# Weights read back in single pieces, two products reordered, and one eviction moved, in a one-core hybrid block

## The chip, the cores and the metric

The kernel runs on one core of a Trainium2 chip. The metric is the device time of one execution in microseconds (us); the time of a kernel is the median of its runs. A core has five engines with queues of their own: PE (TensorE, matrix products; its weight loads are listed as PEld), DVE (VectorE), ACT (ScalarE), POOL (GpSimd) and SP (SyncE, which here only issues transfers). Each engine takes its instructions in the order in which they stand; semaphores order the engines among each other. Products land in PSUM, eight banks of 128 partitions x 512 float32, and have to be copied or added out of it by ACT or DVE before a bank is used again.

## The reference

Everything is float32. The input x is 2 x 2048 x 256. Four residual layers follow each other, each on a layer norm of x:

1. a gated scan: an RMS norm and a 256 x 768 projection give q, kv and a; then s_t = sigmoid(a_t) s_(t-1) + kv_t along the 2048 rows, and q * s is added to x;
2. a feed-forward layer 256 -> 1024 -> 256 with an exact GELU and weights rounded to three values (W1, b1, W2, b2);
3. attention of second order with 16 heads of 64 (q, k, v = x W_q, x W_k, x W_v, each 256 x 1024), a recurrence over the rows, for each head

```
G   = G + k_t (k_t C)        S_K = S_K + k_t k_t'
C   = C + q_t v_t'           o_t = q_t (S_K C - G)
```

   and o W_o is added to x;
4. the feed-forward layer of 2 again, with the same weights.

## The kernel before

The 4096 rows are 32 chunks of 128. The kernel has three parts. `front` does layers 1 and 2 in blocks of four chunks. `attention` does layer 3, and in its last two steps works off the first block of layer 4. The last loop does the rest of layer 4.

**The order** of PE, DVE, ACT and POOL is written out by hand: inside `tc.manual_schedule(engines=by_hand)` an engine's instructions stand in the order in which the Python code makes them. SP's transfers are ordered likewise by when they are made in these parts. Nothing else plans.

**Attention.** A step s is one chunk of one of the two sequences; NS is 32. Steps with even s are `first` (sequence 0), odd s sequence 1; n = s // 2 is the chunk, and `more` is false in the last two steps, 30 and 31. The recurrence is worked chunk by chunk in two stages. `inter` (L887) and `intra` (L901) with q and the running sum S give uT; `products` (L870), masked by DVE (L876), gives the part inside the chunk; `update` (L927) adds the chunk to the running sums S and M; a second `inter` and `intra` with M give oT, two steps later; `outward` (L948) is o W_o, added to x. Stage two needs u also in the other orientation, uN. It is made by DVE's 32 x 32 transposes, a trip through DRAM by SP (`units_out`: one transfer of 512 KB; `turn_rows`: four of 128 KB back), and a copy by ACT (`units_end`, L967, line name uN). kT is made from k in the same way (`keys_out`, `turn_rows`, `turn_end`). All these products have 64 x 64 tiles on PE: one `inter`, `intra` or `products` is 64 matmuls and 64 weight loads.

`evict` (L912 and L914) copies uT or oT out of its two banks with three copies: one of 128 partitions, two of 64. Its argument names the engine, ACT if none is given.

**Seven.** The projections q, k and v of the two sequences' next chunks are done together by Strassen's scheme with seven products, class `Seven`. `go(i)` issues product i and what belongs to it. Three banks are used, X, Y and Z:

| go | bank | after the product |
|---|---|---|
| 2 | Y | |
| 1 | X, new | ACT copies X to C11 |
| 0 | | DVE adds Y to C11 |
| 5 | Z, new | ACT copies Z to C22 |
| 6 | X | ACT copies X to C12 |
| 7 | X | DVE adds X to C22 |
| 3 | Z | DVE adds Z to C12 |
| 4 | X | ACT copies X to C21 |

So 7 waits until ACT has copied what 6 left in X, and 4 until DVE has added what 7 left there. X and Z of q come from a ring of two banks called uT, which uT's own sums use too; those of v from the ring oT; k of step 0 on from uT. Y and all other sums of attention come from a ring of four.

**The weights back.** Layer 4 needs the rounded W1, W2 and their Strassen sums again. `front` wrote them to DRAM, and `ffn_weights_back` reads them with 14 transfers of 256 KB: four for w1 and three for w1_s (`weights(True)`), four for w2 and three for w2_t3 (`weights(False)`). They go over the freed space of wk, wk_t, wv and wv_t and are issued on ACT's queue (L387; names w_back, w_s_back, w_t_back). Each call of `last.part()` issues the next one; `last.part(None)` issues all that are left of the present group. A step has four calls of `last.part()`: before `outward` of step s-3, before the update, in the middle of the second half, and at the end. `weights(True)` stands at the end of step 28, `weights(False)` at the end of step 29.

In steps 30 and 31 `fill(2)` and `fill(1)` put products of layer 4 (L433) between attention's. In step 31 `units(31)` turns u by PE and DVE instead of the trip through DRAM, and uN of step 30 is copied by ACT before the update of M.

Of the kernel before, what the change touches and what calls it, by code (L numbers as in the profile page):

```python
# [43 lines left out]
def kernel(  # L44
# [701 lines left out]
    def attention(keep, pool, state, last):  # L746
# [9 lines left out]
        act, dve = nc.scalar.copy, nc.vector.tensor_copy  # L756
# [105 lines left out]
        def products(s, left, nm):  # L862


            b, n = steps[s]
            banks = [bank([P, NPR, CH], f"h{nm}{b}_{n}_{h}") for h in range(2)]
            for p in range(NPR):
                for c in range(2):
                    for h in range(2):
                        nc.tensor.matmul(  # L870
                            banks[h][halves[c], p, :], lhsT=d[s][left][halves[h], p, halves[c]],
                            rhs=d[s]["qT"][halves[h], p, halves[c]], start=True, stop=True,
                        )
            d[s][nm] = pool.tile([P, 2, NPR, CH], FP, tag=nm, bufs=1, name=f"{nm}{b}_{n}")
            for h in range(2):
                nc.vector.tensor_tensor(d[s][nm][:, h], banks[h], mask8, ALU.mult)  # L876

        def inter(s, sums, nm):

            b, n = steps[s]  # L880
            banks = [bank([P, NPR, CH], f"h{nm}{b}_{n}_{c}", nm) for c in range(2)]
            for p in range(NPR):
                for c in range(2):
                    if d[s][sums][c] is None:
                        continue
                    for h in range(2):
                        nc.tensor.matmul(  # L887
                            banks[c][halves[h ^ c], p, :], lhsT=d[s][sums][c][halves[h], p, :],
                            rhs=d[s]["qT"][halves[h], p, halves[c]],
                            start=(p == 0), stop=False, skip_group_check=True,  # L890
                        )
            d[s][nm + "b"] = banks
# [15 lines left out]
        def evict(s, nm, copy=act):  # L908
            b, n = steps[s]
            banks = d[s][nm + "b"]  # L910
            t = pool.tile([P, NPR, P], FP, tag=nm, bufs=2 if nm == "uT" else 1, name=f"{nm}{b}_{n}")
            copy(t[:, :, halves[0]], banks[0])  # L912
            for h in range(2):
                copy(t[halves[h], :, halves[1]], banks[1][halves[h ^ 1], :, :])  # L914
            d[s][nm] = t
# [47 lines left out]
        def turn_end(s, nm):  # L963

            b, n = steps[s]
            t = pool.tile([P, NPR, P], FP, tag=nm, bufs=1, name=f"{nm}{b}_{n}")
            act(t, d[s]["r" + nm].rearrange("p t q -> p q t"))  # L967
            d[s][nm] = t

        def keys_out(s):  # L970
            turn_squares(s, "kT", d[s]["kN"].rearrange("t (q b i) -> t b q i", q=NPR, b=NQ))
# [4 lines left out]
        def units_end(s):  # L976
            turn_end(s, "uN")
            d[s]["uN"] = d[s]["uN"].rearrange("p a e -> p (a e)")
# [9 lines left out]
        NS = len(steps)  # L988
        pair_sums(0)
        stats = norm_stats(norm_pool, pair(1), bias=True)  # L990
        k, q, v = Seven(0, "kN", "oT"), Seven(0, "qT", "uT"), Seven(0, "vN", "oT")
# [18 lines left out]
        update(0, "kN", "kN", "S")  # L1010
        v.go(6)
        turn_end(0, "kT")
        v.go(7, 3)
        for s in range(NS):
            first, n = s % 2 == 0, s // 2
            more = n + 1 < CPB
            inter(s, "S", "uT")
            products(s, "kT", "p1")
            if first and n + 2 < CPB:
                stats = norm_stats(norm_pool, pair(n + 2), bias=True)  # L1020
            elif s == NS - 4:
                last.stats()
            elif s == NS - 2:
                last.second_stats()
            if s == 0:
                v.go(4)
                pairs[1] = norm_turned(norm_pool, pair(1), xn, bufs=1)
                pair_sums(1)
            if s % 2 == 1 and more:
                q, v = Seven(n + 1, "qT", "uT"), Seven(n + 1, "vN", "oT")  # L1030
            if s == 1:
                q.go(2)
                v.go(2)
                keys_out(s + 1)
            elif s % 2 == 1 and s + 1 < NS:
                keys_out(s + 1)
            if s == 2:
                k = Seven(n + 1, "kN", "uT")
                k.go(2)
            if first and s > 0:  # L1040
                units_end(s - 1)
            last.part()
            if s >= 3:
                outward(s - 3, 1)
            intra(s, "S", "kN", "p1", "uT")
            if s >= 2:
                intra(s - 2, "M", "vN", "p2", "oT")
            if s + 1 < NS:
                turn_rows(s + 1, "kT")
            evict(s, "uT")  # L1050
            if not more:
                if s >= 2:
                    evict(s - 2, "oT")
                last.begin(first)
                fill = last.fill
                fill(2)
                if not first:
                    units_end(s - 1)
                    units(s)
                fill(2)  # L1060
            elif first:
                if s != 2:
                    k = Seven(n + 1, "kN", "uT")
                    k.go(2)
                k.go(1)
                if s >= 2:
                    evict(s - 2, "oT")
                else:
                    units_out(s)
                    turn_rows(s, "uN")  # L1070
                k.go(0, 5)
            else:
                if s >= 2:
                    evict(s - 2, "oT", dve)
                    units_end(s - 1)
                units_out(s)
                turn_rows(s, "uN")
                if n + 2 < CPB:
                    raw = norm_squares(pool, pair(n + 2), [xn], 2, "xraw", 1)
                if s > 1:  # L1080
                    q.go(2)
                    v.go(2)
                q.go(1)
                v.go(1)
                q.go(0, 5)
                v.go(0, 5)
                q.go(6)
                v.go(6)
                if s == 1:
                    units_end(s - 1)  # L1090
            last.part()
            if s == NS - 1:
                last.second_rows()
            if s + 1 < NS:
                update(s + 1, "kN", "kN", "S")
            if s >= 1:
                update(s - 1, "uN", "vN", "M")
            if s == NS - 1:
                update(s, "uN", "vN", "M")
            if first and not more:  # L1100
                turn_end(s + 1, "kT")
            if not more:
                fill(2)
            elif first:
                k.go(*((6, 3, 7) if s > 0 else (6, 7, 3)))
            else:
                v.go(7)
                q.go(7)
                v.go(3, 4)
                q.go(3)  # L1110
            last.part()
            if first and s > 0:
                units_out(s)
            if more:
                turn_end(s + 1, "kT")
            if s >= 1:
                inter(s - 1, "M", "oT")
                products(s - 1, "uT", "p2")
            if not more:
                fill(1)  # L1120
            elif first:
                k.go(4)
                if n + 2 < CPB:
                    xn = norm_rows(norm_pool, pair(n + 2), stats)
                else:
                    last.rows()
            else:
                q.go(4)
            if not first and s + 2 < NS:
                keys_out(s + 2)  # L1130
            if first and s > 0:
                turn_rows(s, "uN")
            if not first and n + 2 < CPB:
                xnT = norm_pool.tile([P, ND, B * P], FP, tag="xnT", bufs=1, name=f"xnT{n + 2}")
                pairs[n + 2] = norm_end(raw, xnT)
                pair_sums(n + 2)
            elif s == NS - 3:
                last.turned()
            if s == NS - 4:
                last.weights(True)  # L1140
            elif s == NS - 3:
                last.part(None)
                last.weights(False)
            last.part()
            if s >= 2:
                outward(s - 2, 0)
        last.out()
# [18 lines left out]
    def pair(n):  # L1166
        return [b * CPB + n for b in range(B)]
# [10 lines left out]
    class Last:  # L1178
# [60 lines left out]
        def fill(self, n):  # L1239
            run(self.steps, n)  # L1240
# [29 lines left out]
    with tc.tile_pool(name="keep", bufs=3) as keep_pool:  # L1270
        with (
# [4 lines left out]
            last = Last(keep_pool, attn_pool)  # L1276
# [68 lines left out]
```

## Time and profile before

| | us |
|---|---|
| median of 3 runs | 1224.65 (1224.0 to 1228.08) |
| profiled execution, its own time | 1226.85 |
| profiled span, first to last instruction | 1224.3 |
| PE busy in the span | 1207.6 |
| DVE, ACT, POOL busy | 785.7, 602.8, 224.9 |

Mean granted clock of PE over the span: 0.999. The front runs to about 308 us, attention from there to about 1038, the rest of layer 4 to the end. Times in the text are microseconds from the span's start. In a row of a timeline the first number is the start, the second the duration, and the bracket at the end is how long the engine had been idle before, and what ended that. In a row of waits the numbers are the total, the count and the longest. "issue" as releaser means that the profile shows nothing that the engine waited for. ACTq and SPq are the queues' own sequencers, issuing transfers.

### The profile page before, as it was taken

To read this page: it belongs to the slowest core of one execution; us is meant where nothing else is said; L and a number is where in the kernel's file an instruction comes from. 1 tells how busy PE (TensorE), PEld (TensorE's weight loads), DVE (VectorE), ACT (ScalarE), POOL (GpSimd) and SP (SyncE) were. 2 spreads that over 40 slices of the span, in tenths; PEclk is the share of its full clock that TensorE was granted. 3 is DMA by queue.
4 is the path that set the end of the run, shared out by engine and by line. 5 is a ranking of instruction groups with operands and counts; after the bars stand their busy time and mean duration, and the time that the engine had idled before them with its cause. 6 is when DMAs were issued, how large, how long until landed. Compare 5 with 4: busy or idle time off the path is not lost.

```text
span 1224.3 us, 46435 instructions
## 1 busy us (share of the span) xinstructions
PE 1207.6 (99%) x21132; PEld 965.6 (79%) x21132; DVE 785.7 (64%) x1283; ACT 602.8 (49%) x953; POOL 224.9 (18%) x363
## 2 busy tenths in 40 slices
PE   9999999999989999999999999999999989999998
PEld 6588777999667777777777777777777878999998
DVE  7966654665466666667666666756766645667764
ACT  4355544453355545454554544455455543455542
POOL 3742143322101100110110011011011100322340
PEclk9999999999999999999999999999999999999999
DMA  9210000000233343233233324323333531112111
GB/s 323 111 61 1 1 1 1 1 2 1 70 123 103 94 139 121 85 129 125 89 106 131 119 87 141 115 83 122 123 103 94 180 109 46 59 63 76 63 53 35
DMA packets 76115, 106.66 MB, mean 87 GB/s; under 512 B 7792, under 2 KB 61808, under 8 KB 75664
## 3 DMA queue, kind: packets, MB, share of 16 engines
q1 hardware_dynamic: 73392, 99.64, 24.3%
q10 hardware_dynamic: 2448, 3.93, 1.1%
q8 instruction: 165, 2.70, 0.9%
q0 software_dynamic: 80, 0.14, 0.1%
q14 instruction: 30, 0.25, 0.1%
HBM read 55.45 MB, written 48.23 MB: 85 GB/s over the span
## 4 chain that ended last, share of the span: by engine, by line
PE 96%; ACT 1%; issue 1%; DMA 1%; DVE 1%; POOL 0%; SPq 0%; ACTq 0%; DVEq 0%; POOLq 0%
PE ox L524 10%; PE hy L948 10%; PE hx L433 9%; PE pq L311 6%; PE hkN_X L816 5%; PE hp L870 5%; PE hqT_X L811 5%; PE hvN_X L816 5%; PE oz L524 5%; PE hz L433 4%; PE huT L887 3%; PE hoT L887 3%; PE huT L901 3%; PE hS L927 3%; PE hoT L901 3%; PE hM L927 3%
## 5 line engine op out<-in xcount | busy, mean ns | idle before, releaser
L876 DVE TENSOR_TENSOR p<-hp,mask 128x512 f32<-128x512 f32 x128 | 82.2, 683 | 95.6 <-PE hp L870 95.6
L948 PE MATMUL hy<-wo,oT 128*128 128x256 f32 x512 | 123.6, 385 | 0.0
L768 POOL TENSOR_TENSOR S<-xnT 128x128 f32<-128x128 f32 x32 | 14.8, 461 | 531.0 <-ACT xnT L255 513.4
L948 PEld LDWEIGHTS hy<-wo,oT 128*128 128x128 f32 x512 | 93.7, 190 | 18.9 <-issue 6.7
L445 ACT ACTIVATE hT<-hT,b_sb 128x256 f32<-128x256 f32 x192 | 85.4, 500 | 33.1 <-DVE hT L477 31.5
L187 ACT ACTIVATE xn<-x_sb,nb,rs 128x256 f32<-128x256 f32 x124 | 64.8, 591 | 69.1 <-POOL nb L173 69.1
L311 PE MATMUL pq<-xnT,wqkva 128*128 128x512 f32 (+1 forms) x216 | 85.0, 547 | 0.6 <-ACT xnT L215 0.3
L912 ACT COPY uT<-huT 128x512 f32<-128x512 f32 x32 | 18.7, 585 | 127.3 <-PE huT L901 127.3
L311 PEld LDWEIGHTS pq<-xnT,wqkva 128*128 128x128 f32 x216 | 39.9, 190 | 37.9 <-issue 34.7
L937 DVE TENSOR_TENSOR S<-S,hS 128x512 f32<-128x512 f32 x60 | 41.2, 687 | 43.9 <-PE hS L927 40.8
L231 DVE STREAM_TRANSPOSE sqkT<-kN 128x1024 f32<-128x1024 f32 x32 | 65.9, 2058 | 1.3 <-ACT kN L847 1.2
L967 ACT COPY kT<-rawkT 128x1024 f32<-128x1024 f32 x32 | 66.6, 2082 | 0.0
L231 DVE STREAM_TRANSPOSE squN<-uT 128x1024 f32<-128x1024 f32 x31 | 63.6, 2051 | 4.0 <-ACT uT L914 3.5
L967 ACT COPY uN<-rawuN 128x1024 f32<-128x1024 f32 x31 | 64.6, 2084 | 1.9 <-issue 1.2
L410 POOL TENSOR_TENSOR xT<-xnT 128x256 f32<-128x256 f32 x15 | 13.6, 907 | 249.2 <-ACT xnT L217 95.7
L530 DVE TENSOR_TENSOR x_sb<-x_sb,ox 128x256 f32<-128x256 f32 x64 | 26.7, 416 | 48.5 <-PE ox L524 48.5
L155 DVE BATCH_NORM_STATS2 st<-x_sb 128x6 f32<-128x256 f32 x128 | 51.3, 402 | 2.5 <-DMA x_sb<-in_x_dram 2.4
L927 PEld LDWEIGHTS hS<-kN 64*64 64x64 f32 x1984 | 32.7, 134 | 23.2 <-issue 23.1
L847 ACT COPY vN<-hvN_X 128x512 f32<-128x512 f32 x16 | 9.4, 586 | 80.7 <-PE hvN_X L816 80.7
L451 ACT COPY hT<-hx 128x512 f32<-128x512 f32 x32 | 18.6, 581 | 61.7 <-PE hx L433 61.7
L821 DVE TENSOR_TENSOR kN<-kN,hkN_Y 128x512 f32<-128x512 f32 x16 | 11.0, 686 | 54.0 <-ACT kN L830 54.0
L901 PEld LDWEIGHTS huT<-p,kN 64*64 64x64 f32 x2048 | 33.2, 134 | 15.0 <-issue 9.2
(245 smaller groups left out, 2929.8 us busy)
## 6 DMA issues: line engine op xcount, KB each, us to landing
dsqkT<-sqkT SPq DMA_DIRECT2D x32, 512.0 KB, 3.3
rawkT<-dsqkT SPq DMA_DIRECT2D x128, 128.0 KB, 2.9
dsquN<-squN SPq DMA_DIRECT2D x31, 512.0 KB, 3.4
rawuN<-dsquN SPq DMA_DIRECT2D x124, 128.0 KB, 3.2
out_dram<-x_sb SPq DMA_DIRECT2D x16, 256.0 KB, 2.2
x_sb<-in_x_dram SPq DMA_DIRECT2D x7, 512.0 KB, 8.9
dsqxn<-sqxn SPq DMA_DIRECT2D x14, 256.0 KB, 3.7
rawxn<-dsqxn SPq DMA_DIRECT2D x56, 64.0 KB, 2.4
```

Source lines behind the costliest of these rows:

```text
L231: nc.vector.transpose(to, src)
L311: nc.tensor.matmul(pq[:, :nt], lhsT=wqkva[:, d, col : col + P], rhs=xnT[:, d, :], start=(d == 0), stop=(d == ND - 1),)
L433: nc.tensor.matmul(at[a][:, j, :], lhsT=A[:, f * P : (f + 1) * P], rhs=Bm, start=(new and j == 0), stop=True, skip_group_check=True,)
L445: nc.scalar.activation(out, out if src is None else src[:, j, :], AF.Gelu, bias=b1_sb[:, f : f + 1])
L524: nc.tensor.matmul(banks[name][:, c, :], lhsT=A[f // 2][:, f % 2, c * P : (c + 1) * P], rhs=Bm[:, f, :], start=(new and c == 0 and f == 0) ...
L816: nc.tensor.matmul(to, lhsT=self.A[i], rhs=self.B[i], start=new, stop=True, skip_group_check=True)
L876: nc.vector.tensor_tensor(d[s][nm][:, h], banks[h], mask8, ALU.mult)
L887: nc.tensor.matmul(banks[c][halves[h ^ c], p, :], lhsT=d[s][sums][c][halves[h], p, :], rhs=d[s]["qT"][halves[h], p, halves[c]], start=(p = ...
L901: nc.tensor.matmul(banks[c][halves[h ^ c], p, :], lhsT=d[s][nat][halves[c], feats(h, p)], rhs=d[s][pm][halves[c], h, p, :], start=(d[s][su ...
L927: nc.tensor.matmul(banks[c][halves[h], p, :], lhsT=d[s][left][halves[c], feats(h, p)], rhs=d[s][right][halves[c], feats(h, p)], start=True ...
L948: nc.tensor.matmul(py, lhsT=d[s]["oT"][:, p, :], rhs=wo[:, p, :], start=(p == 0), stop=(p == NPR - 1),)
L967: act(t, d[s]["r" + nm].rearrange("p t q -> p q t"))
```

## The change

Five edits, all in `attention`. No instruction is added or taken away in total.

- Before step 0, v's products 7 and 3 swap.
- In step 0, k's product 6 moves from behind the update to in front of it.
- In step 1, `units_end(0)` (ACT's copy of uN) moves in front of the evictions of q and v, where it already is in later odd steps; and product 1 of v now comes before product 1 of q.
- In step 31, `evict` of oT of step 29 is done by DVE. In step 30 it stays on ACT.
- In step 29, two more calls of `last.part()`, and the one at the end of the step now comes before `part(None)` and `weights(False)`. The seven transfers of w1 and w1_s then stand one at the end of step 28 and six in step 29: before `outward`, after product 1 of q and v, after product 6, after product 7, after product 3 and 4 of v, and at the step's end. `part(None)` has none left. The first transfer of w2 then stands in the first half of step 30, ahead of `outward`, and each later one a place later than before.

```diff
@@ before step 0
-        v.go(7, 3)
+        v.go(3, 7)
@@ step, last two
-                if s >= 2:
-                    evict(s - 2, "oT")
+                evict(s - 2, "oT", act if first else dve)
@@ step, first and more
                 k.go(0, 5)
+                if s == 0:
+                    k.go(6)
@@ step, odd and more
                 if s >= 2:
                     evict(s - 2, "oT", dve)
-                    units_end(s - 1)
+                units_end(s - 1)
                 units_out(s)
                 turn_rows(s, "uN")
...
-                q.go(1)
-                v.go(1)
+                for part in (q, v) if s > 1 else (v, q):
+                    part.go(1)
+                if s == NS - 3:
+                    last.part()
                 q.go(0, 5)
                 v.go(0, 5)
                 q.go(6)
                 v.go(6)
-                if s == 1:
-                    units_end(s - 1)
             last.part()
@@ after the updates
-                k.go(*((6, 3, 7) if s > 0 else (6, 7, 3)))
+                k.go(*((6, 3, 7) if s > 0 else (7, 3)))
             else:
                 v.go(7)
                 q.go(7)
+                if s == NS - 3:
+                    last.part()
                 v.go(3, 4)
                 q.go(3)
             last.part()
@@ end of the step
             if s == NS - 4:
                 last.weights(True)
-            elif s == NS - 3:
+            last.part()
+            if s == NS - 3:
                 last.part(None)
                 last.weights(False)
-            last.part()
```

## The prediction

> **What bounds the kernel now.** I read the page's busy times and chain first, then the waits of PE (TensorE), then the timelines of PE and ACT round the longest wait, then the DMA traffic of that stretch. From the page:
>
> ```profile
> span 1224.3 us, 46435 instructions
> ...
> PE 1207.6 (99%) x21132; PEld 965.6 (79%) x21132; DVE 785.7 (64%) x1283; ACT 602.8 (49%) x953; POOL 224.9 (18%) x363
> ...
> q8 instruction: 165, 2.70, 0.9%
> ...
> PE 96%; ACT 1%; issue 1%; DMA 1%; DVE 1%; POOL 0%; SPq 0%; ACTq 0%; DVEq 0%; POOLq 0%
> ```
>
> PE is the bound from end to end. The change removes no matmul, so it can only win PE's idle time, or add to it. The waits of PE list nearly all of that (total, times, longest):
>
> ```profile
> PE huT L901 <- issue: 3.3, 1, 3.3
> PE hM L927 <- ACT uN L967: 2.3, 2, 1.5
> ...
> PE hkN_X L816 <- ACT kN L838: 0.8, 1, 0.8
> PE hvN_X L816 <- ACT vN L838: 0.7, 1, 0.7
> ...
> PE hqT_X L811 <- ACT uT L912: 0.7, 1, 0.7
> ```
>
> A "busy" matmul hides some loss, so I measure loss as start-to-start distance beyond that form's usual one. The longest wait stands in step 30 (s = NS-2):
>
> ```profile
> 979.43 1.15 PE L901 MATMUL huT<-p,kN 64*64 64x64 f32 x62
> 983.91 0.27 PE L901 MATMUL huT<-p,kN 64*64 64x64 f32 x1 [3.33 <-issue]
> ...
> 985.10 1.73 PE L433 MATMUL hy<-xnT,w_back 128*128 128x256 f32 x4
> 986.62 1.91 PE L433 MATMUL hx<-xnT,w_back 128*128 128x256 f32 x4
> 988.33 1.32 PE L433 MATMUL hz<-xT_last,w_s_back 128*128 128x256 f32 x4
> 989.48 1.03 PE L433 MATMUL hx<-xT_last,w_s_back 128*128 128x256 f32 x4
> ```
>
> "issue" means that no semaphore held PE. After it, the 128x256 matmuls up to 988.8 stand 427 ns apart instead of 216; the trace has a granted clock of 0.5 for 3.41 us from 985.49. The stall costs 3.54 us by start-to-start distance and the slow clock half of 3.41, 1.7: 5.2 us.
>
> What was late is PE's own instructions. Queue q8 moved 165 packets of 16,384 bytes; 2 x 21,132 PE instructions over 165 is 256 a packet, so q8 is PE's instruction fetch. In the DMA records its packets start after every 260 or so PE instructions (952.77, 956.38, 966.60, 971.92), but the next starts only at 981.47, after 441. Just before it ACT issued five 256 KB weight loads in 2.3 us, and SP 512 KB at 975.21. ACT's queue, then the DMA queues from 973.3 to 981.4:
>
> ```profile
> 973.87 0.33 ACTq L387 DMA_DIRECT2D w_s_back<-dw_s  x1
> ...
> 974.23 0.93 ACTq L387 DMA_DIRECT2D w_s_back<-dw_s  x2
> 975.20 0.44 ACTq L387 DMA_DIRECT2D w_back<-dw  x1
> ...
> 975.78 0.35 ACTq L387 DMA_DIRECT2D w_back<-dw  x1
> ```
>
> ```profile
> DMA packets 848, 1.82 MB, mean 225 GB/s; under 512 B 90, under 2 KB 90, under 8 KB 847
> ...
> q10 hardware_dynamic: 703, 1.29, 50.6%
> q1 hardware_dynamic: 144, 0.52, 16.0%
> q14 instruction: 1, 0.01, 0.2%
> ```
>
> No q8 packet stands in that stretch: the fetch moved when 1.8 MB had drained. Counting 256 instructions back from where PE ran dry, it was due near 976.5, and came some 5 us late.
>
> **The change, part by part.** All against the profiled span of 1224.3.
>
> *v.go(3, 7).* Before, product 6 is followed by 7 into the same bank X, which ACT must first empty: the matmul at 328.42 is 0.75 us late by start-to-start distance. Product 3 writes bank Z, long evicted, and takes 0.95 us, more than the wait. DVE's two additions swap and end as before. Gain 0.75. If that cover failed the 0.75 would stay.
>
> *k.go(6) before the update in step 0.* Product 7 at 341.10 is 0.88 late for the same reason. Now the update's 64 matmuls (1.09) lie between 6 and 7. But 6 now follows 5 at once: its bank X is emptied by ACT at 337.53, or 336.78 after the first gain, and 6 would start at 337.27, so it does not wait. Late next is product 4: X must be freed by DVE's addition of 7, which now queues behind the two S writes (0.66 and 0.69, ending near 340.9), so about 341.5; 4 could start at 341.3. That takes 0.25 back. Gain 0.63.
>
> *Step 1: units_end(0) early, v before q.* q's first product waited 0.88 for ACT to empty a uT bank (349.83); v's bank is free and its product (0.96) covers that. The M update at 357.97 waited 1.74 for ACT's copy of uN. That copy (2.05) now stands ahead of ACT's copies of v and q, and what is queued behind it on ACT is late: with intra at 346.6 (1.4 earlier), uT's copies end at 349.57, uN at 351.62, v's at 352.15, q's at 352.7. PE reaches q.go(6) at 351.35 and waits 1.45 for that bank. Its uN input is there: its four reads were issued from 341.63 and land in about 3 us. So the two waits (2.62) become about 1.7 (1.45 and 0.2 for the second uT bank). Gain 0.88. Bounds: 0.3 if ACT's copies stretch, 1.7 if it hides more. The 0.93 "issue" wait at 378.2 and the 0.84 before huT at 367.46 (q's last copy) are untouched: 0.
>
> *Seven places a step for the weights.* No load is added; 14 of 256 KB remain. Step 29 now has six ordered places (and step 28's end one), so part(None) finds nothing left. ACT's queue gets an issue after the X copies at 960 (0.33 of sequencer, against copies of 0.58 with 0.3 idle after each: covered; uncovered 0.33), two together near 963.3 (ACT is idle for 5.1 us after), one at 969, one at 974; the first w2 load goes behind the uN copy of step 30. The four loads together at 973.87 to 975.64 held ACT for 1.2 us before uN, which has slack (M uses it at 991). SP's and POOL's queues keep their order; of SP's transfers the step-29 reads of uN share the engines with 0.5 MB more, which at 1.82 MB over 6.6 us (975 to 981.5; 275 GB/s) delays them 1.9 us; in before they land near 970 and are used at 975.8. The w2 loads stand a place or so later; first use 1022.5, over 20 us after.
>
> At PE's next fetch, due at 976.5, the engines then hold w1_s's last load, w2's first and SP's 512 KB: 1.05 MB, not 1.8. If the fetch waits for all of it at 275 GB/s, it starts near 979.2, takes 0.94, and as before (982.41 to 983.91) PE resumes 1.5 later, at 981.6, against a run-dry at 980.55: 1.1 us of stall left. If it slips in, none. I take 0.5, the middle, and no slow clock, because PE's other waits of up to 1.5 us left the granted clock at 1. Gain 5.2 - 0.5 = 4.7.
>
> Two rules of the Trainium skill speak against this step. "Runtime: NRT & Kernel Launch", section on instruction fetch mechanics, has the sequencer fetch the next 256-instruction page while it runs the present one, with the cost mostly hidden; "DMA: Bandwidth & Descriptors", section on queues, rings and completion order, lets each DMA engine take turns between queues packet by packet, so that a fetch passes a long queue after one packet (0.1 us in this stretch). By them the burst can't starve PE: the 5.2 stay, and the sum is 3.1 (1221.6). The row is the packet at 981.47 after 441 instructions; I follow it.
>
> *Last eviction of o by VectorE.* In step 31 ACT copies uT, then oT (1.75), then hx, then uN until 1010.86; M at 1010.91 is 0.93 late. With oT on DVE (idle 4.88 us there; the three copies take 2.08, as its own rows at 956.1 show, and end near 1007.8, before hT's addition), ACT copies hx when it exists (1007.5) and uN until about 1010.1. uN's reads were issued from 1001.30 to 1003.87 and land in 3.2, by 1007. Gain 0.8.
>
> **Sum:** 0.75 + 0.63 + 0.88 + 4.7 + 0.8 = 7.8, a span of 1216.5. The profiled execution took 1226.85, 2.2 above the median of 1224.65; I take the same 7.8 off the median: **1216.9**.
>
> **Rivals.** (1) *The fetch was not late because of this burst, or unprofiled runs do not stall there*: for it, the two rules and the 2.2 us between profiled run and median; against it, the one gap in q8 coincides with the burst. It leaves 3.1: 1221.6, within 0.3%. (2) *ACT is the new wait in step 1 and takes the early gains back*: q.go(6) waits for uN. For it, ACT has no gap left there; against it, the old order waits too. Without the 2.3 of steps 0 and 1: 1224.65 - 5.5 = 1219.1. (3) *The starved fetch moves to step 29*, the other side: the fetch at 966.60 now meets 0.5 MB more. It takes 0.88 + 1.5, and PE runs dry at about 971.2, so it may be 2.2 us late before it costs; my estimate is 1.9. Beyond that each us costs one, and near 3.3 idle the slow clock comes with it. If both this stall and the old one stand at 5.2 each: 1224.65 - 3.1 + 5.2 = 1226.8, slower; with a longer drain past 1228.3.
>
> **How the numbers follow.** About 0.3% (3.7 us) is what a measurement tells from no change. Forecast 0.73 and rival 2 0.09 are both faster, 0.82; rival 1 0.12 is same; rival 3 0.06, of which I put 0.05 in slower and 0.01, the cheaper end, in same: 0.13. Range: low end, 5.2 in full, the step-1 bound of 1.7 and the 0.93 fetch wait gone too make 10.0: 1214.6, rounded down to 1214; high end, rival 1 at 1221.6, rounded to 1222.
>
> **What would show it.** In the changed kernel: no 3 us "issue" wait in huT L901 and no 0.5 clock near 980; q8 packets no more than some 300 instructions apart there; ACTq loads single, but for one pair; no waits of hvN_X or hkN_X on ACT; hM in step 31 late by under 0.2; one wait of hqT_X in step 1 near 1.5. Wrong if a new "issue" wait stands at 966 to 972, or step 1 loses over 2.6.

## The result, and the profile after

The changed kernel takes 1219.2 us (median of 7 runs, 1217.3 to 1222.21), the kernel before 1225.38 (7 runs). The two medians differ by 6.2 us. The ratio estimated from all runs is 0.9955, with an interval of 0.9937 to 0.9974: 5.5 us less, between 3.2 and 7.7. Predicted were 1216.9 and 7.8 less. The direction and the range held, and so did the cause named for each part. One term of the sum, that of the weight loads, was too large for most executions, and the picture of how a fetch waits behind transfers was too simple.

From the page of the profiled execution after (its own time 1222.21, 4.6 below that of before):

```profile
span 1220.2 us, 46432 instructions
...
PE 1207.3 (99%) x21132; PEld 965.2 (79%) x21132; DVE 787.5 (65%) x1286; ACT 601.2 (49%) x950; POOL 224.5 (18%) x363
...
PE 97%; DVE 1%; issue 1%; DMA 1%; ACT 1%; POOL 0%; SPq 0%; DVEq 0%; ACTq 0%; POOLq 0%
```

PE's work is the same to 0.3 us, so nearly all of the change is idle time of PE. Queue q8 again has 165 packets. Three copies went from ACT to DVE, the eviction of oT. The waits of PE (total, times, longest):

```profile
PE hoT L901 <- issue: 3.2, 4, 1.4
PE hqT_X L811 <- ACT qT L830: 1.0, 1, 1.0
...
PE huT L901 <- issue: 0.3, 1, 0.3
...
PE hkN_X L816 <- DVE kN L821: 0.3, 1, 0.3
```

The 3.3 us wait of huT is 0.3, and the waits on ACT's kN, vN, uT and uN are gone. In their place stand the two predicted ones: hqT_X on ACT's copy of q, and hkN_X on DVE. Not predicted is the first line, four waits of PE in step 2 (1.02), at 587 and 807 (0.24 and 0.59), and in step 29 (1.37, near 957). In step 30, PE's timeline, then ACT's queue:

```profile
980.88 1.16 PE L901 MATMUL huT<-p,kN 64*64 64x64 f32 x62
982.38 0.21 PE L901 MATMUL huT<-p,kN 64*64 64x64 f32 x1 [0.34 <-issue]
982.39 0.28 PE L901 MATMUL hoT<-p,vN 64*64 64x64 f32 x3
...
983.52 1.13 PE L433 MATMUL hy<-xnT,w_back 128*128 128x256 f32 x4
```

```profile
975.32 0.33 ACTq L387 DMA_DIRECT2D w_s_back<-dw_s  x1
...
975.87 0.33 ACTq L387 DMA_DIRECT2D w_back<-dw  x1
```

Two loads where five stood. The break comes after the same 62 products: the page of instructions ends at the same place, but the next one is there 0.34 us later instead of 3.33. The four products of hy behind it take 1.13, where on the slow clock they took 1.73; the trace has a granted clock of 1 up to the span's last 1.4 us.

**Where the time went, by stage.** I cut the spans at the starts of PE's first huT product of steps 0, 2, 29, 30 and 31, at the first product of attention and at the last product of `outward`. All values are differences of such starts in one profile each; "after, again" is a second profile of the changed kernel:

| stage | before | after | loads alone | order alone | eviction alone | after, again |
|---|---|---|---|---|---|---|
| start of attention to step 0 | 20.00 | 19.15 | 20.00 | 19.14 | 20.00 | 19.15 |
| steps 0 and 1 | 37.13 | 35.55 | 37.13 | 35.53 | 37.13 | 35.53 |
| steps 2 to 28 | 582.56 | 584.38 | 581.82 | 583.77 | 582.25 | 584.13 |
| step 29 | 25.46 | 27.38 | 27.01 | 25.49 | 25.65 | 25.97 |
| step 30 | 23.99 | 19.43 | 19.66 | 22.48 | 22.55 | 19.21 |
| step 31 to the last `outward` | 37.91 | 36.89 | 37.78 | 37.58 | 37.07 | 36.84 |
| span | 1224.3 | 1220.2 | 1221.3 | 1220.6 | 1223.9 | 1217.3 |

The stages in front of and behind these differ by up to about 3 us between executions without any change there. Two columns from one execution each are therefore to be compared by stage, not by span.

Steps 2 to 28 differ as well, though nothing was changed in them. They took 583.8 to 584.7 us in the four profiles with the changed kernel's order of step 1, and 581.8 to 583.7 in the seven with the old order. Whether a part of the early gain is lost there again these single profiles don't settle.

**What the waits named "issue" are.** In the 14 profiles, PE has 109 waits of more than 0.09 us from step 2 on into step 31 for which the profile shows no releaser. Of these, 102 end 2.1 to 2.8 us after the start of a q8 packet, as the 3.33 us wait did (981.47 to 983.91). That marks nearly all of them as late instruction fetches.

### The profile page after: what moved, and what is told of

It reads as the page before. It is cut to its first block, busy times and chain, and to the rows that moved or that the text cites. A ratio compares the mean times of both kernels' runs of the same rounds, so it can differ in the third digit from the quotient of the medians.

```text
span 1220.2 us, 46432 instructions
## 1 busy us (share of the span) xinstructions
PE 1207.3 (99%) x21132; PEld 965.2 (79%) x21132; DVE 787.5 (65%) x1286; ACT 601.2 (49%) x950; POOL 224.5 (18%) x363
## 4 chain that ended last, share of the span: by engine, by line
PE 97%; DVE 1%; issue 1%; DMA 1%; ACT 1%; POOL 0%; SPq 0%; DVEq 0%; ACTq 0%; POOLq 0%
PE ox L524 10%; PE hy L948 10%; PE hx L433 9%; PE pq L311 6%; PE hp L870 5%; PE hkN_X L816 5%; PE hqT_X L811 5%; PE hvN_X L816 5%; PE oz L524 5%; PE hz L433 5%; PE huT L887 3%; PE hS L927 3%; PE hoT L887 3%; PE huT L901 3%; PE hoT L901 3%; PE hM L927 3%
## 5 line engine op out<-in xcount | busy, mean ns | idle before, releaser
L948 PEld LDWEIGHTS hy<-wo,oT 128*128 128x128 f32 x512 | 93.6, 190 | 19.2 <-issue 7.1
L516 DVE TENSOR_TENSOR hS<-hT 128x512 f32<-128x512 f32 x62 | 41.2, 686 | 5.6 <-ACT hT L445 5.6
```

The lines of the kernel that those rows point to most:

```text
L948: nc.tensor.matmul(py, lhsT=d[s]["oT"][:, p, :], rhs=wo[:, p, :], start=(p == 0), stop=(p == NPR - 1),)
```

## The experiments

A diff starts from the kernel before, unless the text names another. Where no ratio is given, the kernel was executed once, and only its profile is used.

**The loads alone.**

```diff
                 q.go(1)
                 v.go(1)
+                if s == NS - 3:
+                    last.part()
...
                 q.go(7)
+                if s == NS - 3:
+                    last.part()
                 v.go(3, 4)
...
-            elif s == NS - 3:
+            last.part()
+            if s == NS - 3:
                 last.part(None)
                 last.weights(False)
-            last.part()
```

> The kernel before with only the change of the weight loads (two more places in step 29, none left for the end of the step). Theory (late instruction fetch behind the burst): the 3.3 us issue wait of huT in step 30 shrinks to under 1 us and the slow clock near 985 goes; minus 3.1 to 5.2 us, less what a new short fetch wait near 957 costs. Rival (fetch and burst have nothing to do with each other): the wait stays near 3 us in the same place, and the time is within 1 us of before.

Measured: 1222.91 (22 runs), ratio to before 0.9978 (0.9972 to 0.9985), so 2.7 us less, 1.8 to 3.4. PE's waits from 320 to 1036 in its profile:

```profile
PE hM L927 <- ACT uN L967: 2.3, 2, 1.5
PE hoT L901 <- issue: 1.5, 2, 1.2
...
PE hkN_X L816 <- ACT kN L838: 0.8, 1, 0.8
PE hvN_X L816 <- ACT vN L838: 0.7, 1, 0.7
```

The long wait of huT is gone and step 30 takes 19.66 instead of 23.99; the early waits stand as before. This alone makes about half of the gain. But step 29 took 1.5 us more in this profile: the issue wait of 1.2 in hoT, near 957.

**The order alone**, before step 0 and in steps 0 and 1.

```diff
-        v.go(7, 3)
+        v.go(3, 7)
...
+                if s == 0:
+                    k.go(6)
...
-                    units_end(s - 1)
+                units_end(s - 1)
...
-                q.go(1)
-                v.go(1)
+                for part in (q, v) if s > 1 else (v, q):
+                    part.go(1)
...
-                if s == 1:
-                    units_end(s - 1)
...
-                k.go(*((6, 3, 7) if s > 0 else (6, 7, 3)))
+                k.go(*((6, 3, 7) if s > 0 else (7, 3)))
```

> The kernel before with only the new order of products and copies in steps 0 and 1. Theory: minus 2.1 to 2.3 us at the start of step 2; the waits on ACT of hvN_X (328), hkN_X (341), hqT_X (350) and hM (358) are gone, one wait of hqT_X on ACT's copy of q (1.0 to 1.5) and one of hkN_X on DVE (0.3) are new; the wait in step 30 stays. Rival (ACT's copy of uN ahead of the others takes it all back): within 0.5 us at the start of step 2.

Measured: 1222.1 (6 runs), ratio 0.9971 (0.9958 to 0.9984), 3.5 us less, 2.0 to 5.1. By stage it is 0.86 and 1.60, 2.5 together, inside that interval. The burst still stands in this kernel, and so does its wait. PE in step 30:

```profile
977.82 1.16 PE L901 MATMUL huT<-p,kN 64*64 64x64 f32 x62
981.11 0.26 PE L901 MATMUL huT<-p,kN 64*64 64x64 f32 x1 [2.14 <-issue]
...
981.28 1.91 PE L901 MATMUL hoT<-p,vN 64*64 64x64 f32 x61
983.11 1.74 PE L433 MATMUL hy<-xnT,w_back 128*128 128x256 f32 x4
```

Same place and same 62 products, but 2.14 us, not 3.33; the clock was at 0.5 from 980.97 to 984.38, so hoT took 1.91 instead of 1.1. So the slow clock also came with a wait of 2.1 us.

**The eviction alone.**

```diff
-                if s >= 2:
-                    evict(s - 2, "oT")
+                evict(s - 2, "oT", act if first else dve)
```

> The kernel before with only the eviction of oT in step 31 on VectorE. Theory: hM in step 31 no longer waits 0.8 us for ACT's uN; minus 0.8 us there, which is less than the timing's own scatter. Rival (uN's reads from DRAM land too late for it): the wait stays, named after uN's DMA.

Measured: 1223.89 (14 runs), ratio 0.9991 (0.9981 to 1.0002): the runs don't tell it from no change. In the profile hM of step 31 starts 0.20 us late instead of 0.93, and the stage takes 37.07 instead of 37.91. Its huT wait in step 30 was 2.16 us.

**The burst moved to step 28.** All seven loads of w1 and w1_s at the end of step 28.

```diff
             if s == NS - 4:
                 last.weights(True)
+                last.part(None)
```

> The kernel before with all seven loads of w1 and w1_s at once at the end of step 28 (1.8 MB), 26 us earlier than its burst of five. Theory: the late fetch moves with the burst: an issue wait of 3 to 6 us and a slow clock between 951 and 960, none over 1 us near 984. Rival (the wait belongs to step 30, not to the loads): 3 us near 984 as before, nothing new near 955.

Half of the expectation failed. Step 30 did as the theory has it (19.68, clock at 1, an issue wait of 0.2). But near 955 the fetch brought a wait of 0.2 only. ACT's queue:

```profile
948.50 2.27 ACTq L387 DMA_DIRECT2D w_back<-dw  x2
...
950.80 2.04 ACTq L387 DMA_DIRECT2D w_back<-dw  x2
957.14 2.07 ACTq L387 DMA_DIRECT2D w_s_back<-dw_s  x3
959.26 0.58 ACT L912 COPY uT<-huT 128x512 f32<-128x512 f32 x1 [8.21 <-DMA w_s_back<-dw_s]
```

And SP's:

```profile
952.51 1.73 SPq L242 DMA_DIRECT2D rawuN<-dsquN  x4
```

The seven did not go out as one burst: four did, the fifth was held to 957.14. The trace shows by what. Transfers of ACT and SP take turns with the same few semaphores, and an issue waits until the transfer that had its semaphore last has landed. The fifth load has the semaphore of the first of SP's four reads of uN; this landed at 957.12, and the load was issued at 957.14. In the same way the fourth load (952.48) followed SP's store of uN, landed at 952.46, and the sixth (957.88) SP's second read, landed at 957.85.

PE's fetch came 4.0 us into step 29 instead of 2.75 in before, and PE had hardly run dry by then. The price came elsewhere: ACT, which takes its instructions in order and was held at these issues, emptied uT late, and hqT_X waited 1.3 us for it. Step 29 took 27.78. The late fetch did not move with the burst, since there was no such burst; the run shows only that without it at step 30, the wait there is gone.

**Four loads, and three.** The kernel before with the first of the two new places, and with both, but with the end of step 29 as it was.

```diff
# four
                 q.go(1)
                 v.go(1)
+                if s == NS - 3:
+                    last.part()
# three: besides
                 q.go(7)
+                if s == NS - 3:
+                    last.part()
```

> The kernel before with one of the two new places in step 29 (after product 1 of q and v), so that four loads instead of five stand in the burst at the end of step 29. Counted from step 30's first huT product, PE's fetch came 4.9 to 6.0 us in after five loads (three profiles), and 2.9 to 3.4 after two (five profiles). Theory (it waits for the loads queued ahead of it, 256 KB at 270 GB/s each): 4.0 to 5.0, an issue wait of 1.2 to 2.2. Rival (a threshold, or the place alone): as with five, or as with two.

> The kernel before with both new places, but the end of step 29 as before, so that three loads stand in the burst. Theory: the fetch 3.3 to 4.1 us after step 30's first huT product, an issue wait of 0.4 to 1.2, and no slow clock. Rival: as with five, or as with two.

Measured: issue waits of huT of 0.98 us with four loads and 1.17 with three.

The start of PE's q8 packet, counted from step 30's first huT product, in all 14 profiles (later experiments included):

| loads in the burst | kernels | fetch, us into step 30 | issue wait of huT, us |
|---|---|---|---|
| 5 | before, order alone, eviction alone | 5.99, 4.97, 4.87 | 3.33, 2.14, 2.16 |
| 4 | one of the places | 3.62 | 0.98 |
| 3 | both places, end as before | 4.01 | 1.17 |
| 2, and a third 0.9 us ahead of them | all seven in step 29, and that with product 4 earlier | 3.35, 2.63 | 0.63, none |
| 2 | after (two profiles), loads alone (two) | 3.10, 2.64, 2.86, 3.26 | 0.34, 0.05, 0.05, 0.45 |
| 2 | burst in step 28, stores, copy of uN between | 2.94, 2.85, 3.22 | 0.21, 0.05, 0.43 |

The cause is shown by this: all three profiles with five loads have a wait over 2 us and the slow clock behind it, and none of the eleven others has either. Neither rival holds: three and four lie between two and five. But three and four don't stand in the expected order, with one profile each, and four lies below what was expected. PE went on 2.2 to 2.5 us after the start of the packet in the burst kernels and in the changed one alike, so the wait follows the fetch. How much of the loads a fetch waits for differs: with five, 1.19 to 1.29 of their 1.31 MB had started when it came, with four only 0.82 of 1.05.

**Stores in place of loads.** To vary the burst elsewhere, the changed kernel got stores of W_o to scratch DRAM at the end of steps 5, 7, 9 and 11. The diff starts from the changed kernel.

```diff
+            for i in range({5: 8, 7: 5, 9: 2, 11: 5}.get(s, 0)):
+                spare = dram.tile([P, 2 * D], FP, tag=f"spare{s}_{i}", name=f"spare{s}_{i}")
+                nc.scalar.dma_start(out=spare, in_=wo[:, 2 * (i % 4) : 2 * (i % 4) + 2, :].rearrange("p c e -> p (c e)"))
             last.part()
```

> The changed kernel with extra stores of 256 KB each (W_o from SBUF to a scratch place in DRAM, never read; no other work changes), issued on ACT's queue in one burst at the end of an odd step: eight in step 5, five in step 7, two in step 9, five in step 11. Steps 6, 8, 10 and 12 have PE's fetch due within 32 instructions of where it is due in step 30. Theory: an issue wait of huT in the first half of the next step, that grows with the burst: under 1 us in step 10, 2 to 3.5 in steps 8 and 12, 4 to 6 with a slow clock in step 6; the q8 packet of each comes when most of the burst has moved. Rival (round robin lets the fetch pass): no issue wait over 1 us in these steps; only ACT may be late by its eight issues.

The expectation missed. PE's waits from 390 to 600:

```profile
PE hoT L901 <- issue: 0.6, 1, 0.6
PE huT L901 <- issue: 0.4, 1, 0.4
```

Behind eight stores (2.1 MB) the fetch of step 6 came 2.62 us in, instead of 1.3 to 1.7 in the other profiles, so about 1.0 late, and cost the 0.4. Behind five it came at 2.43 in step 8, which other profiles show too (1.5 to 2.7), and at 3.47 in step 12 (3.3 to 3.4 in the others; the 0.6 stands here). From 451 to 457 the DMA queues moved 379 GB/s (the prediction's rate for the burst of loads was 275), and ACT needed 6.1 us to issue the eight, so they did not all stand ahead of the fetch when it was due. When the fetch of step 6 started, only half of the stores, 1.06 MB, had. So the number of bytes on the way does not set the delay by itself. Whether loads and stores differ, or only the moment at which they were queued, these runs don't tell.

**The copy of uN between.** In the changed kernel:

```diff
-                units_end(s - 1)
+                if s > 1:
+                    units_end(s - 1)
...
                 v.go(0, 5)
+                if s == 1:
+                    units_end(s - 1)
                 q.go(6)
```

> The changed kernel with ACT's copy of uN in step 1 behind the copies of products 1 and 5 and ahead of those of product 6. Theory: the new wait of hqT_X on ACT's copy of q (1.0 to 1.2 us at 352) goes, and hM does not wait for uN: minus 1.0 to 1.2 us against the changed kernel, so 1218.0 in its median. Rival: the wait only changes its name (hvN_X or hM on ACT), and nothing is won. On the wait of 1.4 to 1.6 us near 957, which the changed kernel and the one with the loads alone both show: it is back if it is caused by the order of the loads, gone if it was chance.

Measured: 1218.68 (6 runs), ratio to before 0.9954 (0.9937 to 0.9971). In its profile the wait of hqT_X is gone and none came for it. Of the waits from 320 to 370, huT on ACT's copy of q (0.7) and product 4 of k on DVE (0.3) are left. Steps 0 and 1 take 34.23 instead of 35.55, 1.3 less, where 1.0 to 1.2 was expected. The median is 0.5 below that of the changed kernel, which these runs don't tell from no difference. There was no wait near 957 (step 29 took 25.64).

**All seven loads in step 29**, on top of that.

```diff
-            if s == NS - 4:
-                last.weights(True)
             last.part()
...
                 if s == NS - 3:
+                    last.weights(True)
                     last.part()
                 q.go(0, 5)
                 v.go(0, 5)
+                if s == NS - 3:
+                    last.part()
...
                 q.go(4)
+                if s == NS - 3:
+                    last.part()
```

> As the kernel with the copy of uN between, and the seven loads of w1 and w1_s all in step 29: none at the end of step 28 and before outward of step 29, two new places after product 5 and after q's product 4. Theory: the two loads at 948 made the fetch late near 957; that wait goes (under 0.3 us), the one near 982 stays under 0.6, and the time falls another 1.4 us against the kernel with the copy of uN between. Rival (the wait near 957 is the fetch behind SP's transfers of uN alone): it stays over 1 us, and the time does not fall.

Measured: 1217.61 (6 runs), ratio to before 0.9943 (0.9925 to 0.9961). Step 29 took 25.46, without a wait; step 30 took 19.75, with an issue wait of 0.6. The expected 1.4 us were not won: the kernel with the copy of uN between had no wait near 957 to lose. So the run doesn't tell the two theories apart, nor do the intervals tell the two times apart.

**q's product 4 earlier in step 1**, on top of that.

```diff
                 v.go(3, 4)
                 q.go(3)
+                if s == 1:
+                    q.go(4)
...
-                q.go(4)
+                if s > 1:
+                    q.go(4)
```

> As the kernel with all seven loads in step 29 and the copy of uN between, and in step 1 product 4 of q ahead of M's inter and products, so that ACT's copy of it no longer stands between q and the next huT. Theory: the wait of huT on ACT's qT at 364 (0.84 by start-to-start distance) goes, minus 0.8 us: about 1216.8 in its median, and faster than both kernels. Rival: kT's copy, which comes after it on ACT, is late instead and takes it back.

Measured: 1218.25 (5 runs), ratio to before 0.9941 (0.9927 to 0.9955). The waits from 320 to 370:

```profile
PE hp L870 <- issue: 1.0, 1, 1.0
PE hoT L901 <- issue: 0.7, 1, 0.7
```

The wait of huT on ACT's qT is gone, kT is not late, and steps 0 and 1 take 33.04, another 1.2 less. But a fetch wait of 1.0 stands right behind, at 365. The median is not below that of the kernel that it starts from. Of these three versions each has a lower median than the changed kernel and none is told apart from it: the intervals overlap.

**Twice more, for the wait near 957.**

> The changed kernel once more, for its profile. Its first profile had an issue wait of 1.4 us near 957 (25.5 us between the first products of steps 29 and 30 became 27.4), as had the kernel with the loads alone; the kernel with the copy of uN between, with the same loads, had none. If the loads' new places cause it: 27 us or more again. If it is chance: it may be 25.5.

> The kernel with the change of the loads alone once more, for its profile. If the loads' new places cause the wait near 957: 27 us or more between the first products of steps 29 and 30, as in its first profile. If it is chance: it may be 25.5. From step 30 to 31: 19.4 to 19.8 in either case.

Step 29 took 25.97 in the changed kernel and 25.46 with the loads alone; step 30 took 19.21 and 19.58. So the same kernels had the long wait near 957 and did not have it; the changed kernel's second profile has 0.2 us there. The moved loads are not its cause, as the order of events in the changed kernel's first profile shows:

```profile
957.19 0.33 PE L901 MATMUL hoT<-p,vN 64*64 64x64 f32 x3 [1.37 <-issue]
```

```profile
947.95 1.13 ACTq L387 DMA_DIRECT2D w_back<-dw  x2
961.26 0.33 ACTq L387 DMA_DIRECT2D w_back<-dw  x1
```

The two loads before the wait go out as in the kernel before (948.41 there), and the first load in a new place comes 4 us after the wait's end. With the loads alone it is the same (957.03 and 961.10).

In the two profiles with the wait, PE's packets had come some 120 to 140 instructions later than in the others already at the fetch before (instruction 36153 and 36132 against about 36015), and the next then came at 36407 and 36433 against about 36290. Why that one came late is open.

## Why the prediction was right, point by point

**PE bound, idle time alone to win.** Right: PE's busy time is 1207.6 before and 1207.3 after.

**v.go(3, 7).** 0.75 predicted, 0.85 measured (20.00 to 19.15), in every kernel that has it.

**k.go(6) and step 1.** 0.63 and 0.88 predicted, 1.51 together; 0.67 and 0.91 measured, 1.58 together (37.13 to 35.55). The prediction's own terms for step 1, 2.62 less 1.45 and 0.2, make 0.97, not 0.88. The two waits that it put in the place of the old ones came, at 0.26 for product 4 of k on DVE (0.25 predicted) and 1.05 for hqT_X on ACT (1.45 predicted). ACT's copies after the change:

```profile
349.62 2.08 ACT L967 COPY uN<-rawuN 128x1024 f32<-128x1024 f32 x1
351.61 0.58 ACT L830 COPY vN<-hvN_X 128x512 f32<-128x512 f32 x1
352.08 0.58 ACT L830 COPY qT<-hqT_X 128x512 f32<-128x512 f32 x1
```

The prediction had uN's end at 351.62 and q's at 352.7. The copy of uN between shows that this stall was not needed: so much of rival 2 is true, but it took back only part of the gain.

**The weight loads.** The cause was right: with the burst gone the fetch comes 2.6 to 3.3 us into step 30, the wait is 0.05 to 0.45, and the slow clock does not come. The 0.5 that was left for a late fetch was also near. The moment at which the fetch was due was not: 976.5 is 1.0 us into step 30, and in no profile did it come before 2.6.

The term that was mis-sized is the 5.2 us for what the burst costs: "The stall costs 3.54 us by start-to-start distance and the slow clock half of 3.41, 1.7: 5.2 us." It was read from one profile, and that was the dearest of three. Step 30 took 23.99, 22.48 and 22.55 with the burst, and 19.2 to 19.7 without it in the four profiles of the changed kernel and of the loads alone, so the burst costs 2.8 to 4.8. Alone, the change of the loads gave 2.7 us in 22 runs, where 4.7 was predicted. That speaks against rival 1 as well: runs without a profile gain too, so they had the stall.

Rival 3 looked for a starved fetch in step 29, at 966 to 972, and none stood there. Two of the six profiles with the loads' new places lost 1.5 to 1.9 in step 29 to a late fetch near 957; but that wait ended before any moved load was issued, and so was not the one that rival 3 feared.

**The two rules set against it.** The packet came 1.6 to 3.4 us later with five loads than with two, and PE stood still for 2.1 to 3.3; so what the Trainium skill says in "Runtime: NRT & Kernel Launch", instruction fetch mechanics, that the fetch is mostly hidden, does not hold in this stretch, where 64 products and their 64 weight loads start in 0.98 us. The turns by packet that "DMA: Bandwidth & Descriptors" gives in its section on queues, rings and completion order are neither shown nor refuted. The prediction took 0.1 us for a turn, which is the time of one packet of 2 or 4 KB in the trace (0.08 and 0.16). A packet on that page is typically 9 to 17 descriptors. If the trace's packets are these descriptors, which no run shows, one turn of both queues is 2.2 to 4.1 us by estimate, about the delay that was measured. The prediction's picture of a fetch that waits until all ahead of it has drained fits the five loads, but not the four, nor the stores: behind eight of them the fetch was only 1.0 late.

**The eviction.** 0.8 predicted; 0.84 in the profile of the eviction alone. hM waits 0.19 after the change, as "under 0.2" had it.

**From the span to the median.** The three changes alone gave 2.7, 3.5 and 1.1, 7.3 together, with wide intervals; all at once 5.5 (3.2 to 7.7). The 7.8 of the sum lies just outside this. In the one pair of profiles, step 30 did give 4.6 us, near the 4.7 of the sum: the prediction was right for the execution that it was read from. With 2.7 for the loads the same sum gives 0.75 + 0.63 + 0.88 + 2.7 + 0.8 = 5.8.

## What to carry to other kernels

An idle stretch of PE that no semaphore explains can be PE's own instructions coming late. Look for the packet of the instruction queue whose start lies some 2 us ahead of the stretch's end, and for a burst of transfers ahead of that packet. Here it was cured by spreading loads that are not urgent singly over the step before. And a stall whose length depends on a race has a size that one profile does not give; take its cost from two or three before it goes into a sum.

When an engine's issue of a transfer is held although its data are ready, see which older transfer had the same semaphore. In the burst moved to step 28 that was a transfer of another engine.

## What the runs showed of the hardware that was not expected

- The slow clock (0.5 for 3.41 us) came with issue waits of 2.1 us in two profiles; waits of 1.0 to 1.5 did not bring it in any.
- The instruction fetch is late now and then throughout attention: "issue" waits of 0.1 to 1.4 us stand in all profiles, and move between executions of the same kernel (step 29 of the changed kernel: 27.4 and 26.0).
- PE goes on 2.1 to 2.8 us after the start of a late packet of 16 KB, in 102 of 109 waits; the late packet of step 30 itself took 0.9 to 1.1 us in all 14 profiles.
